# Two layers of a graph network: other order lists for the first, the middle and the last batches

## The chip, the cores and the metric

The kernel runs on one NeuronCore of one Trainium2 chip. Its engines work side by side, each through its own queue: TensorE (PE: matmuls, and PEld for the weight loads), VectorE (DVE), ScalarE (ACT), GpSimd (POOL) and SyncE (SP), which issues most DMAs. The metric is the time of one execution on the device in microseconds (us), as a median of several.

## The reference

The input x has 32 batches of 512 channels and 1024 points, and adj is a 512 x 512 matrix that serves both layers. All of it is float32.

```python
q = jnp.einsum('c,bcn->bn', wq, x)
k = jnp.einsum('c,bcn->bn', wk, x)
scores = q[:, None, :] + k[:, :, None]
scores = jnp.where(scores > 0, scores, 0.01 * scores)
att = jax.nn.softmax(scores, axis=-1)
agg = jnp.einsum('bcn,bmn->bcm', x, att)
out = jnp.einsum('oc,bcm->bom', adj, agg) + bm[None, :, None]
x = layernorm(x + relu(out))              # layer 0
W = adj * adj
x = layernorm(x + einsum('bnf,nm->bmf', x, W) + bias)   # layer 1
```

The layer norms run over the 1024 points and have no weights.

## The kernel before

**How the work is cut.** One batch fills a tile of 128 partitions x 4 x 1024. The attention isn't computed as a 1024 x 1024 matrix: exp of a leaky ReLU of q + k splits into one factor for each side of the kink, so the kernel sorts the points by q, forms running sums over the sorted rows from both ends, and looks up for each k the two sums at its place. A batch goes through these stages:

- *Query and key.* pa (PE, L221) multiplies x with wq and wk; pc, co and cc copy and transpose the result; ro and rc (L252, L261) spread q over the partitions.
- *Ranks and counts.* rk.b.j (DVE, L271) and ct.b.j (ACT, L284), eight of each; re, ce and we turn them into addresses and weights; oq puts q into the tile zt.
- *z.* z.b.j (PE, L310) is one of eight tiles of adj times x, four float32 matmuls, which the trace shows as 8 records. zc.b.j (ACT, L316) copies it to zt, and sc.b.j (POOL, L324) scatters its rows to the sorted place in DRAM with an indirect DMA.
- *Sums.* sl (SP, L343) loads the sorted rows back in two halves, se (ACT) forms the weights, u.0 to u.7 and d.7 to d.0 (DVE, L362, L372) run the sums upward and downward inside a partition; cu and cd (PE, L380), uc and dc (ACT, L387), tu, td and te (DVE, L405, L414) carry them across partitions. tw (SP, L422) writes the table of both sums to DRAM in two halves, and tl (SP, L425) its last row.
- *Mixing.* g.b.j (POOL, L432) gathers eight tiles of the table; mw (DVE, one for each half of them) needs four gathers landed and forms the weights, ms (ACT, L454) and mx (DVE, L459) mix.
- *Turn and norm 0.* t.b.o (PE, L482) transposes the mix, r.b.o (DVE, L490) adds it to x, s0 (ACT, L468), rt (ACT, L500), rce (DVE) and n0.b.o (ACT, L508) normalise x in place.
- *Layer 1.* A product with W in Strassen and Winograd's manner: t1 to t4 (DVE) form T1 to T4; U, V, Y, Z, 11, 12, 21 are its products on PE (L538 to L575), with copies Uc, Vc, Zc and ll on ACT and additions up and lr on DVE between them. U needs n0.b.0 and n0.b.1. T3 and T4 use tiles 0 to 3 of zt, so they wait for the scatters that read these.
- *Norm 1 and store.* s1 and n (ACT), r1 (POOL), st (SP).

**What sets the order.** No scheduler does. Three lists of words stand in the kernel: `head` is emitted once for the first batches, `loop` once per round for the middle, `tail` for the last batches. A word such as `z.0.4` names a step, its batch (counted from the round's own in `loop`, from 32 in `tail`) and its tile. Each engine runs its own steps in the order of the lists and waits wherever an input isn't there, with everything behind it on that queue.

```python
    def emit(words, base):
        for word in words.split():
            name, b, *at = word.split(".")
            ops[name](base + int(b), *map(int, at))
...
    weights()
    emit(head, 0)
    for b in range(11, B - 7):
        emit(loop, b)
    emit(tail, B)
```

**What is shared.** zt and the tiles tab (sorted rows and table), got and qb exist once; x has four buffers, the PSUM pool of z, sums, carries and queries four, that of turns, pairs and ro two.

## Time and profile before

| | us |
|---|---|
| median of 3 runs (lowest, highest) | 2069.77 (2066.95, 2071.07) |
| the profiled execution | 2069.97 |
| its span | 2068.1 |
| PE busy | 2005.4 |
| DVE, ACT, POOL busy | 1686.9, 1494.8, 848.7 |
| granted PE clock, mean | 0.989 |

A row of the timeline or of the groups gives the start and the busy time in us (or the sum alone), the engine, the line of kernel.py, the operation, what it writes and reads, and how many; in square brackets stands the idle time of the engine before it and what ended it. "q" behind an engine's name is its queue, which issues DMAs. In the text a step is called by its word, with absolute batch numbers (t.6.1 is the turn of tile 1 of batch 6); a time such as "at 475" is counted from the start of the span.

### The profile page before, as it was taken

The numbers are of one execution on the slowest core, as the hardware profiler recorded it, in microseconds if no ns is written. First come the engines' busy times: TensorE is split into PE (matmuls) and PEld (weight loads), VectorE is DVE, ScalarE is ACT, GpSimd is POOL, SyncE is SP. The second block draws the span as 40 slices with busy tenths as digits, with TensorE's granted clock in tenths as the row PEclk, the third lists the DMA queues.
The fourth block names the chain that finished last, engine by engine and source line by source line (L and its number), as shares of the span: only waits on it lengthen the run. The fifth ranks groups of instructions, "written<-read, shape, count | busy, mean of one in ns | idle before, by whom it ended". The sixth has DMA issues, their size and how long they took to land.

```text
span 2068.1 us, 22068 instructions
## 1 busy us (share of the span) xinstructions
PE 2005.4 (97%) x6609; PEld 958.9 (46%) x6609; DVE 1686.9 (82%) x2778; ACT 1494.8 (72%) x2560; POOL 848.7 (41%) x1088
## 2 busy tenths in 40 slices
PE   8999999999999999999999999999999999999976
PEld 4444444444444444544444444444544444444432
DVE  5988888887788888888888888888888888788663
ACT  3567777776777777777787777787777787767666
POOL 4234443453443443443443443443443443444331
PEclk9999999999999999999999999999999999999988
DMA  5568767766677766677766677766677756677752
GB/s 224 199 241 324 286 231 285 311 231 237 247 301 294 291 245 270 246 286 295 296 245 269 246 285 295 287 256 264 250 281 296 301 212 272 240 295 271 275 204 81
DMA packets 137967, 541.04 MB, mean 262 GB/s; under 512 B 14404, under 2 KB 14416, under 8 KB 129656
## 3 DMA queue, kind: packets, MB, share of 16 engines
q1 hardware_dynamic: 80464, 337.47, 41.6%
q0 software_dynamic: 57344, 202.15, 25.3%
q8 instruction: 52, 0.85, 0.2%
q14 instruction: 67, 0.55, 0.1%
q10 hardware_dynamic: 40, 0.02, 0.0%
HBM read 270.29 MB, written 269.29 MB: 261 GB/s over the span
## 4 chain that ended last, share of the span: by engine, by line
PE 71%; DMA 7%; DVE 6%; POOL 3%; ACT 2%; issue 2%; SPq 0%; ACTq 0%; DVEq 0%; POOLq 0%
PE z_ps L310 30%; PE sum_ps L540 16%; PE pair_ps L540 8%; DMA got<-table,of 5%; PE agg_ps L482 5%; PE pair_ps L575 4%; POOL got L432 3%; PE qk_ps L221 2%; DMA table<-end 1%; DVE got L459 1%; PE carry_ps_False L380 1%; DVE tab L405 1%; PE q_tp L252 1%; PE carry_ps_True L380 1%; PE sum_ps L538 1%
## 5 line engine op out<-in xcount | busy, mean ns | idle before, releaser
L310 PE MATMUL z_ps<-adj_t,x 128*128 128x512 f32 x2048 | 908.7, 593 | 2.9 <-ACT zt L316 2.0
L310 PEld LDWEIGHTS z_ps<-adj_t,x 128*128 128x128 f32 x2048 | 382.8, 190 | 441.9 <-issue 430.6
L324 POOL DMA_INDIRECT sorted_z<-zt,to x256 | 327.0, 1277 | 423.7 <-ACT zt L316 323.1
L432 POOL DMA_INDIRECT got<-table,of x256 | 268.8, 1050 | 331.9 <-DVE junk_v L271 117.3
L271 DVE SCALAR_TENSOR_TENSOR junk_v<-qb,qkc,tie 128x1024 uint8<-128x1024 f32 x256 | 328.5, 1283 | 6.0
L284 ACT ACTIVATE junk_s<-qb,qkc 128x1024 bf16<-128x1024 f32 x256 | 294.2, 1149 | 28.8 <-DVE qb L261 20.5
L475 POOL TENSOR_SCALAR var<-var 128x1 f32<-128x1 f32 x128 | 63.4, 496 | 427.0 <-ACT junk L468 411.8
L454 ACT ACTIVATE got<-got,w 128x512 f32<-128x512 f32 x256 | 170.5, 716 | 80.7 <-DVE w L449 61.1
L459 DVE SCALAR_TENSOR_TENSOR got<-got,w 128x512 f32<-128x512 f32 x256 | 185.2, 748 | 40.6 <-ACT got L454 39.2
L316 ACT COPY zt<-z_ps 128x512 f32<-128x512 f32 x256 | 145.5, 580 | 82.5 <-PE z_ps L310 82.2
L490 DVE SCALAR_TENSOR_TENSOR x<-agg_ps,nbm,x 128x1024 f32<-128x1024 f32 x128 | 160.4, 1281 | 17.6 <-PE agg_ps L482 17.4
L372 DVE SCALAR_TENSOR_TENSOR tab<-tab,ac 128x513 f32<-128x513 f32 x224 | 168.7, 753 | 2.7
L405 DVE TENSOR_TENSOR tab<-tab,carry 128x2052 f32<-128x2052 f32 x64 | 146.3, 2291 | 20.7 <-ACT carry L387 20.7
L631 ACT ACTIVATE g<-g,nb,var 128x1024 f32<-128x1024 f32 x128 | 157.6, 1233 | 6.0 <-POOL nb L625 6.0
L468 ACT ACTIVATE junk<-g,tot 128x1024 bf16<-128x1024 f32 x128 | 146.5, 1145 | 19.6 <-DVE g L595 11.9
L468 ACT ACTIVATE junk<-x,tot 128x1024 bf16<-128x1024 f32 x128 | 146.8, 1147 | 18.9 <-DVE x L490 18.0
L540 PE MATMUL sum_ps<-x,adj 128*128 128x512 f32 x256 | 132.7, 642 | 18.9 <-ACT x L508 18.9
L362 DVE SCALAR_TENSOR_TENSOR tab<-tab,ac 128x514 f32<-128x514 f32 x192 | 144.6, 753 | 4.4 <-ACT ac L348 0.9
L482 PE MATMUL agg_ps<-ident,got 128*128 128x128 f32 x1024 | 131.2, 280 | 16.0 <-DVE got L459 8.3
L508 ACT ACTIVATE x<-x,var 128x1024 f32<-128x1024 f32 x128 | 138.3, 1146 | 1.4 <-DVE var L504 1.3
L482 PEld LDWEIGHTS agg_ps<-ident,got 128*128 128x128 f32 x1024 | 116.5, 144 | 48.6 <-issue 17.1
L405 DVE TENSOR_TENSOR tab<-tab 128x1539 f32<-128x1539 f32 (+1 forms) x64 | 129.4, 2025 | 0.8 <-ACT tab L387 0.7
(121 smaller groups left out, 2614.2 us busy)
## 6 DMA issues: line engine op xcount, KB each, us to landing
table<-tab SPq DMA_DIRECT2D x64, 2056.0 KB
tab<-sorted_z SPq DMA_DIRECT2D x64, 1028.0 KB
x<-in_x_dram SPq DMA_DIRECT2D x128, 512.0 KB
out_dram<-g SPq DMA_DIRECT2D x128, 512.0 KB
sorted_z<-zt,to POOLq DMA_INDIRECT x256
got<-table,of POOLq DMA_INDIRECT x256
adj_in<-in_adj_dram SPq DMA_DIRECT2D x1, 1024.0 KB
table<-end SPq DMA_DIRECT2D x32, 2.0 KB
```

Source lines behind the costliest of these rows:

```text
L271: nc.vector.scalar_tensor_tensor(junk, s.qb, s.q[:, j : j + 1], tie[:, at : at + N], ALU.subtract, ALU.is_gt, accum_out=s.rank[:, j : j + 1],)
L284: nc.scalar.activation(junk, s.qb, AF.Sign, bias=s.k[:, j : j + 1], accum_out=s.sign[:, j : j + 1])
L310: nc.tensor.matmul(s.z[j], xt[:, c, j * P : (j + 1) * P], adj_t[:, c, :], start=(c == 0), stop=(c == CT - 1),)
L324: nc.gpsimd.indirect_dma_start(out=sorted_z[b % 2][:, :], out_offset=bass.IndirectOffsetOnAxis(ap=s.to[:, j : j + 1], axis=0), in_=zt[:, j ...
L372: nc.vector.scalar_tensor_tensor(v, v, c, s.zs[:, j + 1, 0:D], ALU.mult, ALU.add)
L405: nc.vector.tensor_tensor(v, v, c, ALU.add)
L432: nc.gpsimd.indirect_dma_start(out=s.got[:, j, :], out_offset=None, in_=table[b % 2][:, :], in_offset=bass.IndirectOffsetOnAxis(ap=s.of[:, ...
L454: nc.scalar.activation(down, down, AF.Copy, scale=s.w[:, 1, j : j + 1])
L459: nc.vector.scalar_tensor_tensor(up, up, s.w[:, 0, j : j + 1], down, ALU.mult, ALU.add)
L468: nc.scalar.activation(junk, t, AF.Square, bias=v[0][:, i : i + 1], scale=-float(N), accum_out=v[1][:, i : i + 1],)
L482: nc.tensor.transpose(s.agg[o][:, j * P : (j + 1) * P], s.got[:, j, o * P : (o + 1) * P], ident)
L540: nc.tensor.matmul(ps, a[:, k, g * P : (g + 1) * P], v[:, k, :], start=False, stop=(k == 1), skip_group_check=first is None,)
```

## The change

The three lists are replaced. The first list now holds 1,653 words instead of 1,541, the last 1,497 instead of 1,609, and the loop's 175 words begin at another step of the round and have an order of their own. The loop's range moves from 11 to 24 to 12 to 25, and makes 14 rounds as before. All in all each step is emitted once for each batch and tile, as before.

The diff, cut to the beginning of the first list, the part around batches 5 to 7, the loop and the range:

```diff
     head = """
-    bias.0 ld.1 ld.2 ld.3 z.0.0 z.0.1 pa.0 z.0.2 pc.0 zc.0.0 zc.0.1 co.0 zc.0.2 pa.1 cc.0 ro.0
-    pc.1 z.0.3 rc.0 rk.0.0 ct.0.5 ct.0.2 rk.0.1 z.0.5 ct.0.3 rk.0.6 zc.0.3 rk.0.4 ct.0.7 z.0.4
-    rk.0.5 ct.0.1 rk.0.7 rk.0.2 z.0.6 zc.0.4 zc.0.5 rk.0.3 ct.0.0 oq.0 re.0 sc.0.4 z.0.7 zc.0.6
...
-    sl.7.0 ct.8.2 Z.5.0 te.6 ct.8.7 rk.8.0 tl.6 sl.7.1 Y.5.0 Zc.5.0 rk.8.3 Vc.5.1 Y.5.1 se.7.0
-    g.6.0 ct.8.1 u.7.0 12.5.0 g.6.2 u.7.1 rk.8.4 se.7.1 g.6.1 Z.5.1 u.7.2 g.6.3 lr.5.0 z.8.0
...
+    bias.0 ld.1 ld.2 ld.3 pa.0 z.0.0 pc.0 co.0 zc.0.0 z.0.1 cc.0 ro.0 zc.0.1 pa.1 rc.0 ct.0.1
+    rk.0.1 z.0.2 ct.0.3 rk.0.7 pc.1 rk.0.2 ct.0.5 z.0.4 rk.0.3 ct.0.2 rk.0.4 ct.0.7 rk.0.6 z.0.6
+    zc.0.4 zc.0.2 rk.0.0 rk.0.5 co.1 zc.0.6 z.0.5 re.0 cc.1 ct.0.4 oq.0 sc.0.1 sc.0.6 z.0.3
...
+    t1.5 tw.6.1 U.5.1 sc.7.2 st.4.3 te.6 t2.5 tl.6 11.5.0 Uc.5.1 Uc.5.0 rk.8.5 ct.8.2 V.5.1
+    rk.8.6 V.5.0 t3.5 Vc.5.1 ct.8.3 rk.8.4 Y.5.1 we.7 rk.8.2 sl.7.0 11.5.1 sl.7.1 t4.5 g.6.0
...
     """
     loop = """
-    Y.-4.1 g.-3.7 up.-4.1 g.-3.5 u.-2.0 21.-4.0 re.-1 ce.-1 u.-2.1 se.-2.1 s1.-4.0 z.-1.0 u.-2.2
...
-    n0.-3.1 tu.-2.1 ro.0 tw.-2.0 n0.-3.3 z.-1.6 n0.-3.0 td.-2.1 t1.-3 U.-3.1 tw.-2.1 zc.-1.6
-    zc.-1.7 rc.0 sc.-1.7 U.-3.0 t2.-3 sc.-1.6 ct.0.1 t3.-3 11.-3.1 ct.0.6 rk.0.1 ct.0.2 Z.-3.1
-    t4.-3 Uc.-3.1 ct.0.5 11.-3.0 rk.0.4 Uc.-3.0 ct.0.3 te.-2 V.-3.1 rk.0.3 tl.-2 ct.0.0 sl.-1.0
...
+    td.-3.1 ro.-1 tw.-3.0 n0.-4.3 z.-2.7 n0.-4.0 tw.-3.1 tl.-3 t1.-4 rc.-1 U.-4.0 rk.-1.7 U.-4.1
...
+    s0.-3.0 sc.-1.1 zc.-1.4 d.-2.0 n.-4.3 sc.-1.4 tu.-2.1 rt.-3 st.-4.3 cd.-2 z.-1.6 dc.-2
+    rce.-3 zc.-1.5 td.-2.0 n0.-3.1 sc.-1.5 n0.-3.2
     """
...
-    for b in range(11, B - 7):
+    for b in range(12, B - 6):
         emit(loop, b)
     emit(tail, B)
```

What the lists make of some queues (only the steps that stand there, in their order):

```text
PE, start          before: z.0.0 z.0.1 pa.0 z.0.2 co.0 pa.1 ro.0 z.0.3 z.0.5 z.0.4
                   after:  pa.0 z.0.0 co.0 z.0.1 ro.0 pa.1 z.0.2 z.0.4 z.0.6 co.1
PE, turns 0        before: z.3.1 z.3.4 z.3.2 t.0.3 t.0.1 t.0.0 t.0.2 z.3.5 cu.1 z.3.3 cd.1 U.0.0
                   after:  z.3.4 z.3.1 t.0.3 t.0.1 t.0.2 t.0.0 z.3.2 cu.1 z.3.3 z.3.5 cd.1 U.0.0
PE, turns 2        before: t.2.3 t.2.2 t.2.0 t.2.1 cd.3 pa.5
                   after:  t.2.3 t.2.2 cd.3 t.2.0 t.2.1 pa.5
POOL, gathers 1    before: r1.0.0 g.1.0 g.1.1 g.1.2 g.1.3 g.1.7 r1.0.1
                   after:  g.1.0 g.1.3 g.1.1 g.1.2 r1.0.1 r1.0.0 g.1.7
DVE, batch 4       before: mx.4.2 u.5.6 ls.3.0 u.5.7 mw.4.1
                   after:  lr.3.1 mx.4.3 mx.4.0 mw.4.1 u.5.5 u.5.6 mx.4.1 u.5.7
SP, tables 5 to 7  before: tw.5.1 st.3.2 tl.5 sl.6.0 ... tw.6.1 st.4.3 st.4.2 sl.7.0 tl.6 sl.7.1 ... tw.7.1 st.5.2 st.5.3 tl.7
                   after:  tw.5.1 st.3.1 sl.6.0 tl.5 ... tw.6.1 st.4.3 tl.6 sl.7.0 sl.7.1 ... tl.7 st.5.2 tw.7.0 tw.7.1
PE, end            before: z.31.7 z.31.6 U.29.0 U.29.1 11.29.1 Z.29.1 V.29.1 11.29.0 V.29.0 12.29.1 Z.29.0 Y.29.1 Y.29.0 21.29.1 12.29.0 21.29.0 cu.31 t.30.3
                   after:  z.31.6 z.31.7 U.29.1 U.29.0 V.29.1 11.29.0 11.29.1 Z.29.1 Y.29.1 Z.29.0 V.29.0 12.29.1 cu.31 21.29.1 Y.29.0 21.29.0 12.29.0 t.30.0
SP, end            before: sl.31.0 tl.30 sl.31.1 st.29.3 tw.31.0 st.29.0 tw.31.1 tl.31
                   after:  sl.31.0 tl.30 sl.31.1 st.29.2 st.29.1 tw.31.0 tl.31 tw.31.1
```

## The prediction

> **What bounds the kernel now.** I read the page's busy rows first, then TensorE (PE) by stage, then what PE waited for.

> ```profile
> PE 2005.4 (97%) x6609; PEld 958.9 (46%) x6609; DVE 1686.9 (82%) x2778; ACT 1494.8 (72%) x2560; POOL 848.7 (41%) x1088
> ...
> PE   8999999999999999999999999999999999999976
> ```

> PE is at 97%, and its two weak slices are the ends. The stage table puts sizes on that (columns: stretch in us, its length, busy us of PE, PEld, DVE, ACT, POOL, then the granted clock, DMA share and GB/s):

> ```profile
> 0.00:140.00 140.00, 129.88 (x480) 64.00 (x481) 111.51 (x192) 76.55 (x141) 58.51 (x84) 1.00 0.54 211
> 140.00:300.00 160.00, 154.23 (x499) 72.80 (x498) 136.72 (x229) 114.98 (x201) 66.14 (x84) 0.99 0.76 292
> 300.00:560.00 260.00, 251.74 (x858) 119.99 (x857) 210.10 (x349) 188.21 (x325) 112.67 (x130) 0.99 0.68 261
> 560.00:1715.00 1155.00, 1154.38 (x3809) 552.42 (x3807) 975.12 (x1597) 869.02 (x1484) 482.54 (x613) 1.00 0.70 273
> 1715.00:1934.00 219.00, 217.82 (x719) 105.29 (x719) 184.03 (x302) 165.04 (x287) 92.97 (x125) 1.00 0.68 262
> 1934.00:2068.00 134.00, 97.32 (x252) 44.37 (x251) 69.40 (x113) 81.03 (x126) 35.90 (x53) 0.86 0.47 177
> ```

> Idle PE time, length minus busy: 10.1, 5.8, 8.3, 0.6, 1.2 and 36.7 us. From 560 on the period is PE's own work; no order can shorten that. An order can win only in the first 560 us and in the last 134. Idle time is not all: after a long gap matmuls run at half clock and still count as busy. I therefore take every step's start-to-start time on PE and subtract its median in the middle of the run (z 3.43 us: 8 records of 0.43; a turn 0.93; pa 1.87; ro 0.87). Steps cost 1979 us in all; before the first z lie 11.0 us; behind the last matmul 11.8; so 66 us of the span are lost in between: 26.6 before 560 us, 35.6 after 1933, 4.0 in between. The largest losses of the head:

> ```profile
> 284.09 5.37 PE L540 MATMUL sum_ps<-zt,S 128*128 128x512 f32 x8 [2.23 <-DVE zt L529]
> ...
> 475.60 3.60 PE L310 MATMUL z_ps<-adj_t,x 128*128 128x512 f32 x8
> 482.98 0.66 PE L482 MATMUL agg_ps<-ident,got 128*128 128x128 f32 x2 [3.79 <-issue]
> ```

> The first is Y of batch 2: 2.2 us of wait, and its 8 records take 5.37 where 8 take 3.60 elsewhere, so 4.2 lost. The second is the turns of batch 6: about 4.0 before them and 3.6 inside, 7.6 lost. Why they are late stands in two queues:

> ```profile
> 435.11 2.51 SPq L636 DMA_DIRECT2D out_dram<-g  x2
> 451.14 0.38 SPq L343 DMA_DIRECT2D tab<-sorted_z  x1
> 451.57 0.35 SPq L425 DMA_DIRECT2D table<-end  x1
> ...
> 456.91 0.97 POOL L432 DMA_INDIRECT got<-table,of  x1 [11.17 <-DMA table<-end]
> ```

> The table's last row (tl.6) stands on SP behind a load (sl.7.0) that waits for the scatters of batch 7; the gathers of batch 6 wait for that row, and mixing and turning wait for them.

> **The change, step by step.** It adds and removes no instruction: the three lists hold the same 5,600 steps, so PE's 1979 us stand. I laid each engine's new order on the durations of before and followed it by hand; times are of the same clock.

> Start. pa.0 (1.87) now precedes z.0.0. The first z's last weight load ends a wait for x at 13.27, so pa.0's last quarter can start only near there; it ends near 13.7, z.0.0 at 17.1. co.0, z.0.1; the column copy stands on DVE behind the bias preparation, which ends at 21.4, so ro.0 runs 21.6 to 22.5. PE has then done 9.8 us of steps: 12.7 lost instead of 11.0, **+1.7**. In return ranking starts at 22.6, not 26.8. What that buys: re.0 is done at 34.7 instead of 38.9, but rc.1 stands behind ro.1 on PE: 46.2 instead of 48.6. The DVE is full from there, and 2.4 us shrink to 1 at the table (td.0.1).

> Turns of batch 0. Before lost 3.4 us here (0.9 and 0.5 between turns, 1.9 before z.3.3, which had no free PSUM buffer since its copy stood behind the root on ACT). The new order puts z.3.2 behind the turns too: turns 120 to 124.5, z.3.2, cu.1, z.3.3, z.3.5, cd.1, U.0.0 at 136.6 against 137.4. So the +1.7 is repaid and **0.8** is won.

> Batches 1 and 2 (up to 240). g.1.* no longer stands behind r1.0.0 on POOL (which held it to 154.6), so DVE doesn't wait at mw.1.0 (1.6), cc.4 comes at 177.8 instead of 181.1, and ro.4 without its 1.0 us wait. At the turns of batch 2 the 2.8 lost shrink to some 1.2, since cd.3 now stands between them. pa.5 at 238.8 against 242.2: **-3.4** in all.

> Y.2.0 at 284. T3 now stands behind two more mixes on DVE: my sum has it at 280.8 with PE ready at 278.7, so 2.1 are lost again. Whether a half clock follows is open. [...] The row says a gap of 2.2 us was enough: 5.37 against 3.60. [...]by the row 3.9; I take the row. Balance at cu.4 **-3.3** [...].

> Batch 4. The gathers start near 321 (before 325.5), as te and tl come earlier. But cu.5 now needs u.5.7, which stands on DVE behind mw.4.1, and that waits for the last gather: the last landed 11 us after its issue before (issued 335.5, mw.4.1 at 347.5), so near 343 now. PE reaches cu.5 at 342.6, u.5.7 is done 3.8 us after mw.4.1: a new wait of 0 to 4.2. Bounds: nothing, if gathers land after 7 us as for the first four; 4.2 and half a clock (1.8) at most. I take 3. t.4.1 then stands 1 to 2 us ahead of 353.2.

> Batches 5 to 7. tl.6 now stands before sl.7.0, behind tw.6.1 and one store. A half table takes 8 to 10 us (in the rest of the run a load into the same tile waits that long behind tw), so g.6.0 starts near 444 instead of 456.9, after sc.7.2 (440). 13 us earlier; mixes end before PE needs them at 474: **-7.6**. The same move for batch 7 (tl.7 before tw.7): -1.5 of the 2.0 lost at 545 to 551. In exchange sl.6.0 stands before tl.5. It waits for tw.5.1 (landed by 384.9) and the scatters of batch 6 (last issued 377), so it frees tl.5 at once: about 0. U.5.1's wait (1.1) came of n.4.2 and an Exp between the norms on ACT; one of the two is still there: -0.5.

> Sum at the loop: 2 and 7.6 and 1.5 and 0.5, some **-11**.

> Loop, 14 rounds. It starts at another step of the round and has its own order. I walked one round: t.3 to t.2 on PE, the residuals, d.0 8.5 to 10.9 us after the first turn, cd at 12.6 (1.7 in hand); n0.0 ends 2.1 before U needs it; the next turns have 1.8 in hand. DVE now waits about 5 us for lr.0, out of some 10 idle per round. No PE wait: 0. tl stands directly behind tw.1, but the table itself lands no sooner.

> End. PE's order in the last three batches is almost the old one; only cu.31 moves up by four steps. Everything hangs on batch 31: last scatter, table, gather, turns, layer 1. There:

> ```profile
> 1941.10 0.38 SPq L343 DMA_DIRECT2D tab<-sorted_z  x1
> 1941.53 0.36 SPq L425 DMA_DIRECT2D table<-end  x1
> ...
> 1957.63 0.17 DVE L445 TENSOR_TENSOR w<-bd,got 128x8 f32<-128x8 f32 x1 [2.49 <-DMA got<-table,of]
> ...
> 1988.49 3.78 PE L540 MATMUL sum_ps<-x,adj 128*128 128x512 f32 x4 [9.54 <-ACT x L508]
> ```

> tl.30 still stands behind sl.31.0, so mw.30.0 stays at 1957.6. From it to the end of tu.31.1 (1986.1) DVE is full: 28.5 us. The new order has u.31.7, lr.29.1 and d.31.7 (1.9) done before, up.29.1 and te.31 (1.4 to 1.9) after: tw.31.1 at 1985.8 to 1986.2, **0 to -0.5**. The wait at U.29 shrinks by 1 (n0.29.0 first), but PE then only waits longer for the turns of batch 30. rt.30 is no longer behind an Exp (one table load of 1.28), but rce.30 still stands behind tu.31.1. The chain from gather to end keeps its links. Two of the four removed waits only change their place, so I set the end at 0, ends -3 and +3. For batches 26 to 29, +1.

> **Sum.** -11 + 0 + 0 + 1 = -10. The profiled execution took 2069.97, the median is 2069.77; 1.9 lie outside the span. Prediction: 2060.

> **Rivals.** (1) The gain goes to new waits in the head: the gathers of batch 4 land late (+4 and 1.8 of half clock, two of which I have), and a like wait comes at batch 5 (+3): 2066 to 2070. For it: DMA at 0.76 of its engines in 140 to 300. Against: tl.6's wait goes whatever else moves. (2) The end gains too: another phase of PE and clock in the last three batches, where 35 are lost, and the head's waits go almost whole (another 5): 2048 to 2055. Against: DVE's 28.5 us have no gap. (3) Slower: the new round isn't free. If one engine's chain misses PE by d in each round, it costs 14 d; the place is rce behind tu.0 and tu.1, or d.0 before cd (1.7 in hand). From d = 0.7 us on it eats the gain, from 1.0 it is slower: 2075. Against: the walk above. (4) The lists don't do what they are called: layer 1 of batch 29 keeps its place on PE; that is true already, and is why I give the end nothing.

> **How the numbers follow.** My case 0.52 (2060, own range 2055 to 2065); (1) 0.20, two thirds of it within the bound; (2) 0.20; (3) 0.08. What a measurement can tell from no change is about 0.2%, 4 us: faster is under 2065.6. Faster: 0.51 + 0.20 + 0.06 = 0.77; same 0.15; slower 0.08. The range leaves out (3) and the depth of (2): 2050 to 2070.

> **What would show it.** First ranks near 28 start 4 us sooner; PE's first gap longer. g.6.0 near 444 and no wait at the turns of batch 6; a wait at cu.5 near 343; loop rounds of 61.9 us with PE full; in the end waits of 9 and 6 us before U of batches 30 and 31 as before. It is wrong if the rounds show waits, if the head keeps over 20 us of loss, or if the last scatter-to-end stretch (133 us) moves by more than 3.

## The result: 2065.6 us, 0.27% faster, about half of what was forecast

The changed kernel takes 2065.56 us (median of 14 runs, 2062.93 to 2068.51); in the same session the kernel before took 2071.02 (14 runs, 2066.95 to 2075.4). The ratio is 0.9973, with a 95% interval of 0.9965 to 0.9982: 5.5 us faster, where 10 were forecast (2060, with a range of 2050 to 2070). The profiled execution took 2065.32 us with a span of 2063.6.

The page's first block, of the changed kernel:

```profile
PE 2004.7 (97%) x6609; PEld 956.7 (46%) x6609; DVE 1674.9 (81%) x2778; ACT 1496.3 (73%) x2560; POOL 874.6 (42%) x1106
...
PE   8999999999999999999999999999999999999976
```

The same table by stage as before (stretch, length, busy us of PE, PEld, DVE, ACT, POOL, granted clock, DMA share, GB/s), the last stretch 4.4 us shorter:

```profile
0.00:140.00 140.00, 130.78 (x481) 63.90 (x482) 111.56 (x193) 76.68 (x142) 62.55 (x82) 1.00 0.54 207
140.00:300.00 160.00, 153.59 (x493) 72.01 (x492) 136.45 (x225) 113.74 (x199) 72.78 (x86) 0.99 0.79 299
300.00:560.00 260.00, 258.37 (x890) 124.25 (x889) 218.10 (x356) 200.30 (x341) 108.82 (x139) 1.00 0.69 267
560.00:1715.00 1155.00, 1151.38 (x3788) 549.60 (x3787) 956.78 (x1597) 862.63 (x1479) 504.80 (x626) 1.00 0.70 273
1715.00:1934.00 219.00, 216.08 (x714) 104.09 (x713) 183.66 (x299) 166.47 (x284) 94.17 (x122) 1.00 0.67 259
1934.00:2063.60 129.60, 94.48 (x249) 42.82 (x247) 68.34 (x112) 76.43 (x121) 31.48 (x52) 0.87 0.45 170
```

Length minus busy PE: 9.2, 6.4, 1.6, 3.6, 2.9 and 35.1 us, where before had 10.1, 5.8, 8.3, 0.6, 1.2 and 36.7. The gain lies in 300 to 560. Against the forecast, 140 to 300 got worse, and the loop, which ran with 0.6 us idle, now has 3.6.

The lines that answer those shown of before: Y of batch 2, then the turns of batch 6 (PE's timeline), and the SP queue and the first gather behind it:

```profile
286.44 2.81 PE L540 MATMUL sum_ps<-zt,S 128*128 128x512 f32 x6 [0.51 <-DVE zt L529]
...
478.70 1.03 PE L380 MATMUL carry_ps_True<-end,before 128*128 128x257 f32 x4
479.57 1.91 PE L482 MATMUL agg_ps<-ident,got 128*128 128x128 f32 x16
```

```profile
440.20 0.33 SPq L422 DMA_DIRECT2D table<-tab  x1
440.63 0.39 SPq L636 DMA_DIRECT2D out_dram<-g  x1
442.07 0.24 SPq L425 DMA_DIRECT2D table<-end  x1
449.71 0.93 SPq L343 DMA_DIRECT2D tab<-sorted_z  x2
...
450.50 1.32 POOL L432 DMA_INDIRECT got<-table,of  x1 [8.23 <-DMA table<-end]
```

The table's last row goes out at 442.1 instead of 451.6, the gathers start at 450.5 instead of 456.9, and both turns run back to back (16 records in 1.91 us) without the 7.6 us of loss. The end keeps its chain, 4 to 5 us earlier throughout:

```profile
1937.24 0.37 SPq L343 DMA_DIRECT2D tab<-sorted_z  x1
1937.66 0.36 SPq L425 DMA_DIRECT2D table<-end  x1
...
1953.32 0.17 DVE L445 TENSOR_TENSOR w<-bd,got 128x8 f32<-128x8 f32 x1 [2.88 <-DMA got<-table,of]
...
1983.63 3.78 PE L540 MATMUL sum_ps<-x,adj 128*128 128x512 f32 x4 [8.82 <-ACT x L508]
```

One profile of each order isn't enough to split 5 us by stage: waits of a us or two come and go from one execution to the next (between 560 and 1715 the profiles of one order lost from 2.6 to 7.5 us). The experiments below repeat each order in part, so every stretch was profiled several times. This table adds up the loss of all steps on PE in each stretch (start to start, minus the step's median, as in the prediction; the first row includes the time ahead of the first step; the last one leaves out the step that begins just ahead of 1934, which the forecast's 35.6 for the end includes). Behind each mean stand the kernels that have that order in that stretch.

| stretch, us | old order, us lost | new order, us lost | difference | forecast |
|---|---|---|---|---|
| 0 to 140 | 17.0 (before, e2, e3: 15.4, 18.9, 16.7) | 14.4 (after, e1, e4, e6, e7, e10, e11, e12: 14.2 to 14.6) | -2.6 | -0.8 |
| 140 to 300 | 8.7 (the same: 8.9, 8.5, 8.6) | 11.5 (the same: 10.5 to 12.9) | **+2.8** | **-2.5** |
| 300 to 560 | 13.2 (before, e2: 13.3, 13.1) | 5.8 (after, e1, e6, e7, e12: 3.5 to 7.3) | -7.4 | -7.7 |
| 560 to 1715 | 2.8 (before, e1, e3, e9, e11, e13: 2.3 to 3.8) | 4.6 (after, e2, e4, e5, e7, e10: 2.6 to 7.5) | **+1.8** | **0** |
| 1715 to 1934 | 4.9 (before, e1, e3, e11, e13: 3.7 to 6.0) | 3.9 (after, e2, e4, e5, e6, e10: 2.5 to 5.4) | -1.0 | +1 |
| from 1934 | 32.0 (the same: 31.5 to 32.4) | 32.8 (the same: 31.3 to 33.9) | +0.8 | 0 |
| sum | | | -5.6 | -10 |

The sum meets the measured 5.5 us. Nearly all that is missing lies in two rows: batches 1 to 3, and the loop.

### The profile page after: what moved, and what is told of

Read it like the earlier page. It is cut to its first block, busy times and chain, and to the rows that moved or that the text cites. A ratio compares the mean times of both kernels' runs of the same rounds, so it can differ in the third digit from the quotient of the medians.

```text
span 2063.6 us, 22066 instructions
## 1 busy us (share of the span) xinstructions
PE 2004.7 (97%) x6609; PEld 956.7 (46%) x6609; DVE 1674.9 (81%) x2778; ACT 1496.3 (73%) x2560; POOL 874.6 (42%) x1106
## 2 busy tenths in 40 slices
PE   8999999999999999999999999999999999999976
## 5 line engine op out<-in xcount | busy, mean ns | idle before, releaser
L310 PE MATMUL z_ps<-adj_t,x 128*128 128x512 f32 x2048 | 906.6, 593 | 0.4 <-ACT zt L316 0.4
L310 PEld LDWEIGHTS z_ps<-adj_t,x 128*128 128x128 f32 x2048 | 384.1, 190 | 448.0 <-issue 439.5
L324 POOL DMA_INDIRECT sorted_z<-zt,to x256 | 377.2, 1473 | 481.0 <-ACT zt L316 403.7
L432 POOL DMA_INDIRECT got<-table,of x256 | 262.2, 1024 | 209.6 <-issue 87.8
L284 ACT ACTIVATE junk_s<-qb,qkc 128x1024 bf16<-128x1024 f32 x256 | 293.9, 1148 | 18.9 <-DVE qb L261 17.0
L475 POOL TENSOR_SCALAR var<-var 128x1 f32<-128x1 f32 x128 | 46.3, 362 | 461.9 <-ACT junk L468 458.6
L459 DVE SCALAR_TENSOR_TENSOR got<-got,w 128x512 f32<-128x512 f32 x256 | 180.9, 745 | 10.9 <-ACT got L454 10.7
L631 ACT ACTIVATE g<-g,nb,var 128x1024 f32<-128x1024 f32 x128 | 157.8, 1238 | 11.8 <-POOL nb L625 11.8
L405 DVE TENSOR_TENSOR tab<-tab,carry 128x2052 f32<-128x2052 f32 x64 | 144.8, 2292 | 11.5 <-ACT carry L387 11.5
L540 PE MATMUL sum_ps<-x,adj 128*128 128x512 f32 x256 | 131.4, 637 | 16.3 <-ACT x L508 16.3
L482 PE MATMUL agg_ps<-ident,got 128*128 128x128 f32 x1024 | 133.4, 278 | 11.2 <-issue 4.7
L508 ACT ACTIVATE x<-x,var 128x1024 f32<-128x1024 f32 x128 | 138.5, 1149 | 0.7 <-DVE var L504 0.6
L601 DVE SCALAR_TENSOR_TENSOR g<-sum_ps,g 128x512 f32<-128x512 f32 x64 | 44.0, 687 | 111.8 <-ACT junk_s L284 75.3
L482 PEld LDWEIGHTS agg_ps<-ident,got 128*128 128x128 f32 x1024 | 115.2, 143 | 36.3 <-DVE x L490 12.2
```

Source lines behind the costliest of these rows:

```text
L284: nc.scalar.activation(junk, s.qb, AF.Sign, bias=s.k[:, j : j + 1], accum_out=s.sign[:, j : j + 1])
L310: nc.tensor.matmul(s.z[j], xt[:, c, j * P : (j + 1) * P], adj_t[:, c, :], start=(c == 0), stop=(c == CT - 1),)
L324: nc.gpsimd.indirect_dma_start(out=sorted_z[b % 2][:, :], out_offset=bass.IndirectOffsetOnAxis(ap=s.to[:, j : j + 1], axis=0), in_=zt[:, j ...
L432: nc.gpsimd.indirect_dma_start(out=s.got[:, j, :], out_offset=None, in_=table[b % 2][:, :], in_offset=bass.IndirectOffsetOnAxis(ap=s.of[:, ...
L459: nc.vector.scalar_tensor_tensor(up, up, s.w[:, 0, j : j + 1], down, ALU.mult, ALU.add)
L482: nc.tensor.transpose(s.agg[o][:, j * P : (j + 1) * P], s.got[:, j, o * P : (o + 1) * P], ident)
```

## The experiments

All of them only change the order of the 5,600 steps, except where it is said otherwise. The kernel before was run beside each group; its medians there were 2072.56 (e1 to e4), 2071.74 (e5, e6, e7, e9) and 2071.52 (e10 to e13). Kernels of different groups are compared by their ratios to it.

### e1_head and e2_rest: which half holds what

The two orders meet at a point where every engine's order agrees but for one step, so that they can be joined there.

```diff
 e1_head
-    all steps in the changed order
+    steps 1 to 1600 in the changed order, all others in the order of before
 e2_rest
-    all steps in the changed order
+    steps 1 to 1642 in the order of before, all others in the changed order
```

> The changed order for the first 1,600 steps (up to about 602 us), from there on the order of before; at the seam every engine's order is the old one but for a single step of VectorE. Theory A (the forecast's head was about right, and what is missing went in the loop): the head's -9 to -10 stays, the rounds of the loop run without a wait: 9.5 us faster than before, and no loss at the second turn of any batch from 9 to 25. Theory B (the head gave only some 5 us; the waits that the loop shows come from the head's state and appear with either loop): 5 us faster, with such waits still there.

> The reverse: the order of before for the first 1,642 steps (up to about 624 us), from there on the changed one. Theory A: loop +4.6 and batches 26 to 28 +0.4, end -1: 4 us slower than before, with waits at the second turn in about half of the rounds. Theory B: the loop is neutral of itself and the end gives 1: from 1 us faster to the same.

Measured: e1_head 2064.06, ratio 0.9957 (0.9945 to 0.9970), 8.9 us faster. e2_rest 2072.26, ratio 1.0000 (0.9992 to 1.0009). So the gain is the head's, and everything behind it brings nothing; B's guess of 5 us for the head is below the interval of e1_head (6.2 to 11.4 us). A's guess of +4 for the rest is refuted: e2_rest's interval ends at 1.9 us slower. In e1_head no second turn of a batch from 9 to 25 lost over 0.3 us; in e2_rest two did (0.4 and 0.5), in the changed kernel six (0.5 to 1.2). The loop's waits therefore belong to the changed loop, but a cost of 4.6, as the two profiles at hand then had it, was their bad end. The two parts, 8.9 and 0, don't add up to the 5.5 of the whole change (interval 3.7 to 7.2); the intervals are wide enough to allow it.

### e3_tl6_alone and e4_tl6_undone: the one large step

```diff
 e3_tl6_alone (against before)
-    ... rc.8 tw.6.1 st.4.3 ... sl.7.0 ct.8.2 Z.5.0 te.6 ct.8.7 rk.8.0 tl.6 sl.7.1 ...
+    ... rc.8 tw.6.1 te.6 tl.6 st.4.3 ... sl.7.0 ct.8.2 Z.5.0 ct.8.7 rk.8.0 sl.7.1 ...
 e4_tl6_undone (against after)
-    ... te.6 t2.5 tl.6 11.5.0 ... sl.7.0 11.5.1 sl.7.1 ...
+    ... te.6 t2.5 11.5.0 ... sl.7.0 tl.6 11.5.1 sl.7.1 ...
```

> Before with one thing of the change: te.6 and tl.6 (the table's last row of batch 6) stand directly behind tw.6.1, ahead of the load sl.7.0. By the forecast's step the gathers of batch 6 start near 444 us instead of 456.9 and the 7.6 us at the turns of batch 6 go: 7 us faster. Rival: the gathers were late for another reason (the landing of tw.6.1, the scatters of batch 7 on the same queue): gathers start at 452 or later, 0 to 3 us faster.

> After with that one thing undone: tl.6 directly behind sl.7.0. By the forecast's step 7 us slower than after, so about 1.5 us slower than before. Rival: the rest of the new order has slack for it, 0 to 3 us slower than after (2.5 to 5.5 us faster than before).

Measured: e3_tl6_alone 2067.78, ratio 0.9983 (0.9973 to 0.9993), 3.5 us faster. e4_tl6_undone 2070.36, ratio 0.9992 (0.9984 to 1.0000), 1.7 us faster than before, so some 3.9 slower than after. Both lie between the theories. In e4 the waits at the turns of batch 6 are back (6.8 us in the steps from cu.7 to t.6.0). So the step is worth 3.5 to 3.9 us of the kernel's time, not the 7.6 lost at those turns. In e3 these waits are gone and the gathers start at 446.9 instead of 456.9, ten us earlier, but part comes back as new waits a little ahead. PE's timeline of e3_tl6_alone:

```profile
464.36 1.98 PE L540 MATMUL sum_ps<-zt,adj 128*128 128x512 f32 x4 [0.73 <-DVE g L601]
468.58 1.98 PE L540 MATMUL pair_ps<-x,S 128*128 128x512 f32 x4 [2.24 <-ACT g L585]
```

The copy that releases the second (L585) stands on ScalarE right behind the Exp of the next batch's loaded rows. That Exp for the second half of the load (se.7.1) comes at 467.6 instead of 459.3, though it was issued only 0.8 us later. In e3 the gathers started before the load had gone through, and the load's second half was used 8.3 us later. This price wasn't in the forecast, and it returns in e5 and e7 below.

### e5_tl_head: the failed term of batch 1

In the changed order the table's last row of batch 1 stands behind the load of batch 2 on SP, where before it stood ahead of it. The changed kernel, on SP, POOL, DVE, and then PE:

```profile
154.01 0.37 SPq L343 DMA_DIRECT2D tab<-sorted_z  x1
154.44 0.35 SPq L425 DMA_DIRECT2D table<-end  x1
154.83 0.37 SPq L343 DMA_DIRECT2D tab<-sorted_z  x1
...
160.05 0.97 POOL L432 DMA_INDIRECT got<-table,of  x1 [15.49 <-PE sum_ps L540]
...
172.28 0.17 DVE L445 TENSOR_TENSOR w<-bd,got 128x8 f32<-128x8 f32 x1 [4.48 <-DMA got<-table,of]
...
179.84 0.44 PE L236 MATMUL qk_tp<-ident,part 128*128 128x128 f32 x2 [3.24 <-ACT part L229]
180.11 5.29 PE L310 MATMUL z_ps<-adj_t,x 128*128 128x512 f32 x8
185.24 1.04 PE L252 MATMUL q_tp<-ident,qkc 128*128 128x128 f32 x8
```

Gathers of batch 1 from 160.1 (before 156.7), weights of the mix at 172.3 (169.2). The copy that co.4 needs (pc.4) stands on ScalarE behind four mixing scales of batch 1, and PE loses 3.5 us waiting for it. Another 1.7 go ahead of ro.4, which the expectations below call a wait at ro.4. The rows show none there: the 8 records of z.4.4 take 5.29 us, and the trace grants half the clock from 180.57 on, for 3.41 us. So the 5.2 us are the one wait at co.4 and the half clock behind it.

```diff
-    ... t2.0 tw.1.1 ce.2 V.0.0 t3.0 Zc.0.0 ... te.1 Vc.0.0 ... sl.2.0 tl.1 ...
+    ... t2.0 tw.1.1 te.1 ce.2 V.0.0 t3.0 tl.1 Zc.0.0 ... Vc.0.0 ... sl.2.0 ...
-    ... uc.2 mw.1.0 ... r.1.3 tw.2.0 ... st.0.3 ct.4.2 te.2 ... sl.3.0 tl.2 ...
+    ... uc.2 te.2 mw.1.0 ... r.1.3 tl.2 tw.2.0 ... st.0.3 ct.4.2 ... sl.3.0 ...
-    ... ct.7.3 te.5 Z.4.0 ... sl.6.0 Z.4.1 tl.5 sl.6.1 ...
+    ... ct.7.3 te.5 tl.5 Z.4.0 ... sl.6.0 Z.4.1 sl.6.1 ...
```

> After, with the table's last rows of batches 1, 2 and 5 (te and tl) ahead of the load of the next batch (sl.2.0, sl.3.0, sl.6.0), behind which the changed lists put them. Theory: tl.1 behind sl.2.0 is what makes the gathers of batch 1 start at 160.1 (before 156.7) and the 5.2 us at co.4 and ro.4 follow from it through ScalarE's queue: those waits go, and some 1 us at the turns of batch 5 with them, 5 to 6 us faster than after, 11 us faster than before. Rival: the gathers wait for the table's half tw.1.1 or for the engines of the DMA, which are busy with other loads: gathers start no sooner than 159, 0 to 2 us faster than after.

Measured: 2064.23, ratio 0.9963 (0.9950 to 0.9977), 7.7 us faster than before; against after that is 2 us, inside both intervals. The gathers start at 154.8 as the theory said, and co.4 doesn't wait, but PE then waits 4.9 us at cu.2, for the last running sum of the next batch. SP, ScalarE and PE of e5_tl_head:

```profile
145.49 0.23 SPq L425 DMA_DIRECT2D table<-end  x1
154.08 0.92 SPq L343 DMA_DIRECT2D tab<-sorted_z  x2
...
159.63 0.30 ACT L348 ACTIVATE ac<-tab,top 128x4 f32<-128x4 f32 x1 [5.04 <-DMA tab<-sorted_z]
166.99 0.30 ACT L348 ACTIVATE ac<-tab,top 128x4 f32<-128x4 f32 x1 [6.87 <-DMA tab<-sorted_z]
...
171.46 2.08 PE L380 MATMUL carry_ps_True<-end,before 128*128 128x257 f32 x4 [4.92 <-DVE end L362]
```

The load goes out at the same time (154.1), but its second half is used at 167.0, where the changed kernel has 162.1 (the same line of its timeline reads 162.07, idle 2.22). The 5.2 us from co.4 to ro.4 became 7.2 from cu.2 to pa.4, again a wait (4.9 us) and a slow stretch behind it: the next record of z (L310) takes 1.06 us, where the page's mean is 0.59. The theory's first step held, its last did not: here the row's place only decides which of two transfers is late.

### e7_tl30 and e9_best: the same at the end

```diff
 e7_tl30 (against after)
-    ... te.-2 tw.-2.1 ... sl.-1.0 Uc.-3.0 tl.-2 sl.-1.1 ...
+    ... te.-2 tw.-2.1 tl.-2 ... sl.-1.0 Uc.-3.0 sl.-1.1 ...
 e9_best
+    steps 1 to 1600: order of e5_tl_head; all others: order of before,
+    with tl.30 directly behind tw.30.1
```

> After, with tl.30 directly behind tw.30.1, ahead of the load sl.31.0 that waits for the last scatters. Theory: g.30.0 starts some 5 us sooner (1938 instead of 1943), mw.30.0 with it, and the chain from there to the end (mixes, tu.31.1, table, gather, turns, layer 1 of batch 31) moves up: 4 us faster than after, 9.5 us faster than before. Rival: the chain to the end hangs on sl.31.0 and the sums of batch 31 (u.31), which the earlier gathers only slow down: 0 to 1 us faster than after, or slower.

> The three parts that should be good together: the changed order of the head with the rows tl.1, tl.2 and tl.5 ahead of the loads, from step 1,600 on the order of before, and in it tl.30 ahead of sl.31.0. If all parts add up: head -8.5 and -5, loop 0, end -4: 17 us faster than before. If the parts only pass their waits on: 8 to 10 us faster.

Measured: e7_tl30 2071.98, ratio 1.0000 (0.9993 to 1.0007), 5.6 us *slower* than after by the ratios; e9_best 2069.32, ratio 0.9987 (0.9979 to 0.9994), 2.7 us faster than before and slower than e1_head. In e7 the rival had the direction right, but not the size. In e9 both guesses missed (17 us, and 8 to 10): the moved row took back at the end most of what the head had won. e7_tl30 on SP, ScalarE, DVE and PE:

```profile
1929.14 0.24 SPq L425 DMA_DIRECT2D table<-end  x1
...
1937.67 0.93 SPq L343 DMA_DIRECT2D tab<-sorted_z  x2
...
1946.97 0.30 ACT L348 ACTIVATE ac<-tab,top 128x4 f32<-128x4 f32 x1 [5.68 <-DMA tab<-sorted_z]
1954.34 0.30 ACT L348 ACTIVATE ac<-tab,top 128x4 f32<-128x4 f32 x1 [6.41 <-DMA tab<-sorted_z]
...
1958.80 0.17 DVE L445 TENSOR_TENSOR w<-bd,got 128x8 f32<-128x8 f32 x1
...
1958.34 2.08 PE L380 MATMUL carry_ps_True<-end,before 128*128 128x257 f32 x4 [6.25 <-DVE end L362]
```

The row goes out 8.5 us earlier than in the changed kernel (1929.1 for 1937.7) and the first gather starts 7.5 us earlier (1935.8 for 1943.3). The load of batch 31, issued at the same time, is then used at 1947.0 and 1954.3, where the changed kernel has 1942.9 and 1945.5. The last sum ends at 1958.3 instead of 1949.8, the weights of the mix follow on the same engine at 1958.8 instead of 1953.3, and the end is 6 us later. So the row that stands behind sl.31.0 isn't a fault of the order: it holds the gathers back until the load is on its way.

### The loop: e6_loop_mix and e12_gathers_behind_load

In the changed loop the gathers of a batch start 0.3 us after the last scatter of the next one, ahead of the load; in the loop of before they wait for the last row and start 1.6 us behind the load. Two rounds of the changed kernel, the first with a wait, the second without: SP, ScalarE (the Exp of the loaded rows) and, in the first, PE at the second turn.

```profile
638.12 0.93 SPq L343 DMA_DIRECT2D tab<-sorted_z  x2
...
649.49 0.30 ACT L348 ACTIVATE ac<-tab,top 128x4 f32<-128x4 f32 x1 [5.89 <-DMA tab<-sorted_z]
...
666.62 1.64 PE L482 MATMUL agg_ps<-ident,got 128*128 128x128 f32 x13 [0.82 <-DVE got L459]
```

```profile
699.53 0.92 SPq L343 DMA_DIRECT2D tab<-sorted_z  x2
...
706.65 0.30 ACT L348 ACTIVATE ac<-tab,top 128x4 f32<-128x4 f32 x1
```

The last scatters end at 634.5 and 697.7. From there to the Exp are 15.0 and 9.0 us. The sums, the mixing weights and the mixes follow on DVE almost without a gap; in the first round the last mix ends 1.3 us behind the start of the first turn, in the second 2.0 ahead of it. In the loop of before the Exp stands late in ScalarE's queue (15.0 us after the scatter in each of 17 rounds), so that a late load is covered, and the last mix ends 1.4 ahead every time.

```diff
 e6_loop_mix
-    ... u.-2.7 n.-4.1 mx.-3.6 d.-2.7 ms.-3.5 st.-4.1 oq.-1 d.-2.6 ms.-3.4 z.-1.2 ms.-3.7 mx.-3.4
+    ... u.-2.7 mx.-3.6 ms.-3.5 oq.-1 ms.-3.4 z.-1.2 ms.-3.7 n.-4.1 st.-4.1 mx.-3.4
-    ... st.-4.0 mx.-3.3 cu.-2 ...
+    ... st.-4.0 mx.-3.3 d.-2.7 d.-2.6 cu.-2 ...
 e12_gathers_behind_load
-    ... tw.-3.1 tl.-3 t1.-4 ... g.-3.3 sl.-2.0 t4.-4 we.-2 sl.-2.1 V.-4.1 g.-3.2 ...
+    ... tw.-3.1 t1.-4 ... g.-3.3 sl.-2.0 t4.-4 we.-2 sl.-2.1 tl.-3 V.-4.1 g.-3.2 ...
```

> After, in each round of the loop the last mixes earlier: d.7 and d.6 behind the last mix instead of among them, and the norm n.-4.1 behind the mixing scales on ScalarE. The mixes end some 1.3 us sooner. Theory: in about a third of the rounds the load of the sorted rows lands some 3 us late and the last mix then misses the second turn by 0.5 to 1.5 us; with 1.3 us more in hand nearly all of these waits go: 3 to 4 us faster than after (9 us faster than before). Rival: the second turn waits for something else, or d.5 to d.3 come late for cd instead: the same as after, or slower.

> After, in each round of the loop tl.-3 behind the load sl.-2.1, so that the gathers can't start before the load has gone out. If the gathers' transfers are what makes the load late: the Exp of the loaded rows comes 9 to 10 us after the last scatter in all rounds (in after 9.0 to 15.0), and the gathers and mixes come some 8 us later, so that PE waits 3 to 6 us at the turns of each round: 40 to 80 us slower. If the load is late of itself: the Exp keeps its spread of 9 to 15 us.

e6_loop_mix: 2066.25, ratio 0.9969 (0.9957 to 0.9980). In its profile the last mix ends up to 4.5 us ahead of the turn in quiet rounds (in after up to 3.1) and about 1 ahead in most late ones (in after 1 behind), and one second turn from batch 9 to 25 still waits (1.3 us), where the six profiles of the changed loop have 2 to 6. So the cause of these waits is the one named, the late last mix; but 3.6 us are lost between 560 and 1715, where the six have 2.6 to 7.5, and the time can't be told from that of after. The expected 3 to 4 us rested on one bad profile; the rival's "the same as after" holds for the time, though not for its reason.

e12_gathers_behind_load missed its aim. Three of a batch's eight gathers stand ahead of the row's new place in the list; they don't wait for it, they read the table before its last row is written, and the row then waits for them. So gathers and load still ran side by side, the other gathers stood behind the row, and PE waited in all rounds: 2164.89 us, in a single run. The Exp came 9.1 to 13.9 us after the scatter. This settles neither theory for the loop.

### e10_tl5, e11_tl5_old_rest and e13_parts4: what is left to win

```diff
 e10_tl5 (against after)
-    ... ct.7.3 te.5 Z.4.0 ... sl.6.0 Z.4.1 tl.5 sl.6.1 ...
+    ... ct.7.3 te.5 tl.5 Z.4.0 ... sl.6.0 Z.4.1 sl.6.1 ...
 e11_tl5_old_rest
+    steps 1 to 1600: order of e10_tl5; all others: order of before
 e13_parts4 (against e11_tl5_old_rest)
-    ... uc.2 mw.1.0 ... g.1.6 pa.4 d.2.4 ... d.2.3 pc.4 mx.1.2 d.2.2 co.4 z.4.4 ... ms.1.4 cc.4 ms.1.6 ...
+    ... uc.2 pa.4 pc.4 mw.1.0 ... g.1.6 d.2.4 ... d.2.3 co.4 cc.4 mx.1.2 d.2.2 z.4.4 ... ms.1.4 ms.1.6 ...
```

> After, with tl.5 alone moved: directly behind te.5, ahead of the load sl.6.0. Of the three rows moved together before, this is the one behind which the waits at the turns of batch 5 (1 to 2.5 us) went away, while tl.1 only moved a wait from co.4 to cu.2. Theory: 1 to 2 us faster than after (7.5 us faster than before). Rival: the load sl.6.0, now beside the gathers, makes the sums of batch 6 and cu.6 late instead: the same as after.

> The head of the run before this one, and from step 1,600 on the order of before (a second comparison of the two orders of the loop behind one and the same head). If the changed loop costs 3 us by its waits: 3 us faster than the run before this one, 10 us faster than before. If the loop's cost was chance: the same as the run before this one within 1.5 us.

> As the second run of this call, and pc.4 directly behind uc.2 on ScalarE (ahead of the mixing scales of batch 1), cc.4 ahead of mx.1.2 on VectorE. If the waits at co.4 and ro.4 (about 4 us) are nothing but queue order: they go, the turns of batch 1 then wait for the last mix at most 2 us, and it is 2 us faster than that run. If the gathers of batch 1 bind there anyway: the wait turns up whole at t.1.3, 0 us.

Measured: e10_tl5 2062.60, ratio 0.9951 (0.9938 to 0.9965); e11_tl5_old_rest 2061.96, 0.9949 (0.9935 to 0.9962); e13_parts4 2061.62, 0.9948 (0.9934 to 0.9961). All three beat both kernels: 10 to 11 us faster than before, and the intervals of the last two end below that of after (0.9965 to 0.9982); that of e10_tl5 touches it. So one step moved, tl.5, is worth some 4.5 us by the ratios, where 1 to 2 were expected, or chance has a share in it. In its profile the waits at the turns of batch 5 (1.6 us in after, 1.9 to 3.1 in e7, e6 and e1) are gone, and the load sl.6.0, which had its scatters done, pays nothing; t.4.1 waits 1.7 instead. e10 and e11 agree within 0.7 us: behind this head the choice of the loop makes no difference that these runs can tell.

In e13_parts4 nothing is lost from co.4 to ro.4, and 3.9 us turn up in the three steps from cd.2 to t.1.3, a wait of 2.0 and a slow stretch behind it (8 records of z in 4.37 us, 3.60 elsewhere):

```profile
183.80 1.04 PE L252 MATMUL q_tp<-ident,qkc 128*128 128x128 f32 x8
186.87 2.05 PE L380 MATMUL carry_ps_False<-tab,behind 128*128 128x257 f32 x4 [2.03 <-issue]
188.71 4.37 PE L310 MATMUL z_ps<-adj_t,x 128*128 128x512 f32 x8
192.92 1.26 PE L482 MATMUL agg_ps<-ident,got 128*128 128x128 f32 x10
```

The mixes of batch 1 now come later (the last one ends at 191.5, in e11 at 189.7), since their scales stand behind pc.4 on ScalarE. But this profile can't credit the edit with the missing wait at co.4. Its PE had already lost 4.4 us between 154 and 163, ahead of the edited steps, where e11 lost nothing; the profiles of e1, e6 and e10 lose 2 us or more there too, without that edit. co.4 starts at 180.1 in e13 and at 180.2 in e11, and at 179.5 to 181.2 in all profiles of the new order that leave tl.1 in its place. So moving pc.4 made nothing earlier that these profiles can show. Whether the gathers alone bind there, as the rival says, stays open.

## Why the forecast came out at half its gain

The path was the right one: the change acts through SP's queue, the table's row and the gathers, and PE's own work stands. The size failed, in one step above all.

**Start (-0.8): right, and a little too small.** U.0.0 was forecast at 136.6 and ran at 136.5. The new order lost 14.2 to 14.6 us up to 140 in every profile; the old one 15.4 in the profile that was read and 18.9 and 16.7 in two others.

**Batches 1 and 2 (-3.4 with the start, so -2.6 of their own): wrong, this is the step that failed.** It said that the gathers of batch 1 no longer stand behind r1.0.0, and that cc.4 comes at 177.8. r1.0.0 did move, but the gathers didn't start earlier: the step read POOL's queue and not SP's, where tl.1 had moved behind sl.2.0. It was the very pattern that the prediction had found at batch 6, with the sign turned round. cc.4 came at 182.9, pa.5 at 245.2 for 238.8, and the stretch costs 2.8 us more than before, not 2.5 less. e5_tl_head shows that the obvious repair would not have saved the term: with the gathers ahead of the load, its second half was used at 167.0 instead of 162.1. The sum has two small slips besides: from -3.4 on, 3.9 lost at Y.2.0 for 4.2 would make -3.7 and not -3.3, and the four terms at the loop add up to 11.6 and not 11.

**Y.2.0 (2.1 to 3.9 lost again): too dark.** It lost 0.7 in each of the changed kernels, with a gap of 0.5 us, so the question whether a half clock follows was not put there. The old head put it twice more: in e2_rest and e3_tl6_alone the gap was 1.6 us and the 8 records took 3.70, where before had 2.2 and 5.37. The last section sets such gaps beside the granted clock.

**Batch 4 (a new wait of 3 at cu.5): right in kind, too large.** It was 0.7 us in after and 1.5 to 2.3 in the others.

**Batches 5 to 7 (-7.6, -1.5, -0.5): right at the turns of batch 6; that the whole stretch from 300 on meets its -7.7 is luck in part.** Measured -7.4 by the profiles' losses, with the new wait at cu.5 and with 1.6 us at the turns of batch 5 that hadn't been seen: tl.5 behind sl.6.0, which the prediction set at "about 0" since that load's scatters were done. The gathers of batch 6 started at 450.5 and not at 444, because PE, and with it tw.6.1 (440.2), was later after the lost term; they were still in time. By the kernel's time the move of tl.6 is worth 3.5 to 3.9 us (e3, e4).

**Loop (0): off by +1.8.** The walk through one round was right for a quiet round: the last mix 1.3 to 3.1 us ahead, no wait. It used each duration once. The load's time has a spread (Exp 9.0 to 15.0 us after the last scatter) that the old order hid behind ScalarE's queue, and the new one doesn't. This is the mechanism of rival (3), not in each round by d, but in two to six rounds by 0.3 to 1.3.

**Batches 26 to 29 (+1) and the end (0): -1.0 and +0.8.** They cancel as the forecast's sum had it. The chain from the last scatter to the end is indeed unchanged; and tl.30 behind sl.31.0, which looked like its flaw, is what keeps it short.

Of the three signs of being wrong that the forecast named, two came. The rounds show waits, and the head keeps 21 us of loss in the mean of the profiles (18 in the changed kernel's own), where the limit was 20. The last scatter-to-end stretch didn't move by more than 3: 130.8 us, 132.5 before.

Of the rivals, (1) is the nearest, and the measured time lies between its 2066 to 2070 and the case's own 2055 to 2065: the head's gain went to new waits in part, though more at batch 1 than at batches 4 and 5. (4) was true, as was said. (2) is refuted for the end: with the step just ahead of 1934, 35 us were lost there before, 33 to 35 after.

## What to carry to other kernels

When a reordering frees a transfer, list everything that is then in flight with it: here a small row that "stood in the way" was the gate which let a load go ahead of eight gathers, and opening the gate was worth 3.5 to 3.9 us at one batch (7.6 at its turns, in part paid back), nothing at another, and minus 6 at the end. Check the pattern that explains the largest gain at every place where it occurs, with its sign; the term that failed was the same one at another batch. And a walk with one duration for each step shows the quiet round: ask which of its durations has a spread, and whether the old order hid it.

## What was not expected of the hardware

The late loads of the loop are not spread at random. The page has a small queue:

```profile
q8 instruction: 52, 0.85, 0.2%
```

It is 52 transfers of 16 KB, one each 37 us (median). Which engine they serve, no trace here shows.

In the six profiles of the changed loop there are 102 rounds. In 21 of them such a transfer starts within 2 us of the end of the last scatter: there the load is issued 3.3 us after the scatter and its Exp runs 14.1 us after it (medians), and 17 of the 21 lose over 0.3 us at the turns. In the other 81 the load is issued after 1.8 us, the Exp runs after 9.6, and 2 lose. The two rounds shown above are one of each. The DMA of 5 us around the last scatter of the first, 632.5 to 637.5:

```profile
q0 software_dynamic: 190, 0.65, 44.5%
q8 instruction: 1, 0.02, 2.4%
```

The same stretch of the second, 695.7 to 700.7, has no such transfer. The 21 aren't independent cases: they are the rounds of batches 9, 12, 20 and 23, and at 20 only in three profiles. In the other three the transfer of that round began 2.6 to 2.7 us ahead of the scatter's end; its Exp ran after 10.0 to 13.1 us instead of 14.3 to 14.8, and no turn lost over 0.3. So the four rounds aren't late for their place alone. Nor does every late turn come with one: the 2 of the 81 are rounds 16 and 22 of the changed kernel, one of them with the largest loss of its profile (1.2).

The kernel before has the same 52 transfers, and its rounds take 61.9 us each. In the changed loop the load went out 1.5 us later, and its Exp ran 4.5 us later, in the 21 rounds than in the 81. In the six profiles of the old loop 10 of 102 rounds have such a transfer so near, and their load goes out 6.4 us after the scatter instead of 5.1; the Exp, at 15.0 in any case, covers it. That the two go together is shown by the counts; that the transfer makes the load late is not, and how it would do so stays open, since no run moved a transfer alone.

A load with gathers beside it was later than expected, and by the same at three places: the second half of a load (1028 KB) was used 7.4 us after the first in e3_tl6_alone, e5_tl_head and e7_tl30, where it was 2.7 to 3.1 in the kernel before and in the changed one there.

| without a matmul in a window at full clock | windows | followed by half clock |
|---|---|---|
| under 1.5 us | 8,110 | 0 |
| 1.5 to 2.0 us | 33 | 8 |
| 2.0 us and more | 74 | 74 |

A window already at half clock was followed by another in 72 of 72 cases with 0.8 us or more without a matmul, and in 2 of 84 with less. This answers what the forecast left open at Y.2.0. The gap of 2.23 us in the kernel before (281.87 to 284.10) lay almost whole in the window that ends at 284.08; the gap of 1.6 us there in e2_rest and e3_tl6_alone can't reach 2.0 wherever the windows fall, and no half clock followed (8 records in 3.70 us). In a forecast a wait of 2 to 4 us is therefore, as an estimate from these counts, a chance of a second loss, since two windows may share it, and the row of one profile shows it as yes or no.
